# Four half units per expert job beside the first layer, and a larger TensorE share with more blocks for the experts beside the last attention

## The chip, the cores and the metric

The kernel runs on one core of a Trainium2 chip. The metric is the device time of one execution in microseconds. Before the change the median of three runs is 14575.84 us (14560.78 to 14577.56).

Each engine works through its own queue in the order in which the program was written: TensorE (PE; its weight loads are shown apart as PEld), VectorE (DVE), ScalarE (ACT), GpSimd (POOL), and SyncE (SP), which here issues nearly all the DMAs. An instruction that must wait holds up everything behind it on its engine.

## The reference

The input x has 4 entries of 32 x 96 tokens with 256 channels, all in float32. An entry therefore has 3072 tokens, and there are 12288 in all. What is computed:

```python
x = x + conv(group_norm(x))              # layer 0: two Mamba blocks, one along the 96, one along the 32
t = tokens(x)                            # (4, 3072, 256)
n = layer_norm(t)                        # additive attention within an entry:
h = tanh(n @ Wt [:, :, None] + n @ Wx [:, None] + bh)     # 3072 x 3072 x 32 of each entry
t = t + softmax(h @ Wa + ba) @ n
y = layer_norm(t)                        # expert layer:
gates = top2_softmax(graph_attention(y @ W_gat, edges))   # 1048576 edges over all 12288 tokens
for e in range(4):
    t = t + gates[..., e] * (gelu(y @ W1[e] + b1[e]) @ W2[e] + b2[e])   # 256 -> 512 -> 256
```

The product with the gates comes last. So an expert's output for a token (before its gate) can be computed as soon as that token's attention is done, kept in DRAM, and added when the gates are known.

## The kernel before

**Stages.** The order of the work on PE, ACT, DVE and POOL is written out by hand: Python generators are stepped in turn, and the order in which they emit instructions is the order in each engine's queue. First layer 0 of entry 0 runs alone. Then layer 0 of entries 1 to 3 runs beside the attention of entries 0 to 2. Then the attention of entry 3 runs beside the sorting and counting of the graph's edges (`Edges.sort`) and the first expert work (`Experts.early`). Last comes `tail`: the rest of the graph and of the experts.

**Columns, slots, blocks.** The attention (`Attention.units`) does one column at a time: ACT takes a tanh of 128 x 3072 (L1036), and PE multiplies it with Wa two columns later (L1009, the scores). There are three tanh buffers, so a tanh waits until the scores of the one three columns earlier are done. Eight columns make a unit of 32 queries; then an exponential, transposes and the product with the values follow. An entry has 768 columns. Layer 0 works in blocks of 384 tokens with 48 slots, one slot per column (`Layer0.run`). In each column the generators are stepped in two halves.

**A unit of expert work** is 512 tokens (a block, 24 in all, 6 per entry) by one expert; 96 in all. PE multiplies with W1 in four parts of 128 features, two matmuls each, then a GELU follows, and PE multiplies with W2. There are three places for it.

*`Beside`* works beside layer 0, on entries 0 and 1. A job is three half units (256 tokens each) of one expert and takes one block of layer 0; the table `PRODUCTS` says in which slot the two halves of a hidden product are issued, `GELU` in which slot the one GELU over all three (128 x 3072) is, `OUTPUTS` where the products with W2 are. Each product writes to the same single PSUM bank (`bank`, tile `ex`); DVE empties it in the next slot. The expert's weights and tokens lie in the key and query buffers (`krep`, `qsel`) that the attention will need for the next entry, so a job can start only while those are free. `choose` takes a job at the end of a block, if the entry's attention is past column 12, the keys of the next entry aren't asked for, and the tokens are of an entry that is normalized and older than the one whose attention runs. An entry has 12 half blocks and 4 experts: 16 jobs of three.

*`Experts.early`* works beside the last attention. It takes what `Beside` left of entries 0 to 2, two units of one expert at a time, with one GELU per unit (128 x 2048). It is a generator that yields after each small piece what that costs in the planner's microseconds (0.95 for a hidden matmul, 1.85 for a part of an output, 2.0 for the GELUs, 4.0 for a change of the expert). The loop in `whole` grants a credit in each column:

```python
us_t = min(us_t, SLOT_US) + SLOT_US - att.extra
```

where `att.extra` is what the attention's own tail steps cost in this column (0.7, 0.4 and 2.9 in three of eight). The credit first pays for one batch of the edge counting products (8 x 0.11), then for pieces of expert work as long as it is positive. `early` starts once entry 2 is wholly normalized, some 17 columns into the last attention. After the attention the pair that has begun is ended.

*`tail`* does the remaining units, and among them the graph: 384 row gathers by POOL, scores, scatter products (L1666) of 120 groups, and the gates of each quarter (entry) in the order 2, 0, 3, 1. Its planner lays everything out in half steps, six to a unit; it counts a half step with a unit as 2.7 us and one without as 0.5, a gather as 1.6 and a group as 2.0. For a block whose outputs were kept, the outputs of all four experts are read back (1 MB for half a block) and added with their gates (L1995), in blocks spaced by 2 or 3 times two half steps once its gates are ready.

The lines of the profile that matter: L1824 and L1835 (products of `Beside`), L1830 (its GELU), L1811 and L1816 (DVE emptying its bank), L1910 and L1918 (products of `early`, with `krep`, and of `tail`, with `w`), L1954 (GELU of `early`), L1992 (GELU of `tail`), L1265 (gathers) and L1601 (POOL's waits for DVE's marks that pace them).

Of the kernel before, what the change touches and what calls it, by code (L numbers as in the profile page):

```python
# [26 lines left out]
P = 128  # L27
# [4 lines left out]
KC = C // P  # L32
# [34 lines left out]
KO_BUFS = 2  # L67
SLOT_US, PRODUCT_US = 1.2, 0.11
EU, EG = 32, 2
# [771 lines left out]
class Attention:  # L841
# [4 lines left out]
    def __init__(self, ctx, tc, ident, a, x1, x2, xn2T, tab_s, tab_a, keys, l0):  # L846
# [30 lines left out]
        self.extra, self.entry, self.col, self.asked, self.normed = 0.0, 0, 0, 0, 0  # L877
        self.now, self.reduces, self.more, self.tc = None, False, [], tc
        self.mark = const.tile([P, 1], F32, tag="mark", name="mark")
# [320 lines left out]
    def after(self, b, t0=0, t1=NT):  # L1200
# [7 lines left out]
        for j in range(j0, N):  # L1208
# [27 lines left out]
            if b < B - 1:  # L1236
                nc.sync.dma_start(self.tab_e[:, n0:n0 + CT, :], hb)
            nc.sync.dma_start(self.tab_a[b][:, j * CT:(j + 1) * CT, :], db)
            if j == NT // CT - 1:
                self.normed = b + 1  # L1240
# [509 lines left out]
class Beside:  # L1750
# [4 lines left out]

    PRODUCTS = {0: (0, 0), 3: (0, 1), 5: (1, 0), 8: (1, 1), 10: (2, 0), 12: (2, 1)}
    GELU = 14
    OUTPUTS = {15: (0, 0), 17: (0, 1), 20: (1, 0), 23: (1, 1), 26: (2, 0), 29: (2, 1)}

    def __init__(self, ctx, tc, a, l0, att, xn2T, dram):  # L1760
# [6 lines left out]
        self.half = TB // 2  # L1767
        n = TOK // self.half // 3
        self.jobs = [(b, e, j) for b in range(B - 2) for e in range(NEXP) for j in range(n)]
        self.kept, self.done, self.job, self.there = {}, [], None, None  # L1770

    def units(self):

        halves = {(2 * (b * TOK // TB) + 3 * j + k, e) for b, e, j in self.done for k in range(3)}
        return [(i, e) for i in range(NBLK_X) for e in range(NEXP)
                if (2 * i, e) in halves and (2 * i + 1, e) in halves]

    def choose(self, last):
# [8 lines left out]
        place = att.krep[(att.entry + 1) % 2]  # L1787
        self.w1, self.w2 = expert_places(place)
        rest = att.qsel[(att.entry + 1) % 2]
        self.xt, self.b2 = rest[:, :KC * self.half].rearrange("p (k m) -> p k m", k=KC), rest[:, KC * self.half:]  # L1790
        if self.there != (att.entry, e):
            self.there = att.entry, e
            load_expert(self.nc, self.a, e, self.w1, self.w2)
            self.nc.sync.dma_start(self.b2, self.a["b2_rep"][:, e, :])
        self.first = 2 * (b * TOK // TB) + 3 * j
        self.fetch(0)

    def fetch(self, k):
        m = (self.first + k) * self.half
        self.nc.sync.dma_start(self.xt, self.xn2T[:, :, m:m + self.half].rearrange("k p m -> p k m"))  # L1800

    def __call__(self, slot, last):
        nc = self.nc
        if self.job:
# [3 lines left out]
            if slot - 1 in self.PRODUCTS:  # L1808
                k, f2 = self.PRODUCTS[slot - 1]
                for f in (2 * f2, 2 * f2 + 1):  # L1810
                    nc.vector.tensor_scalar(self.h[:, k, f, :], self.ps[:, f % 2, :],  # L1811
                                            self.b1[:, e, f:f + 1], None, ALU.add)
# [18 lines left out]
            if slot in self.OUTPUTS:  # L1831
                k, q = self.OUTPUTS[slot]
                self.ps = self.bank()
                for f in range(FC):
                    nc.tensor.matmul(self.ps[:, 0, :], self.h[:, k, f, q * P:(q + 1) * P],  # L1835
                                     self.w2[:, f, :], start=(f == 0), stop=(f == FC - 1))
# [14 lines left out]
class Experts:  # L1851
# [3 lines left out]
    def __init__(self, ctx, tc, x2, xn2T, gates, out, dram, beside=None):  # L1855
# [5 lines left out]
        self.kept, self.done = (beside.kept, beside.units()) if beside else ({}, [])  # L1861
        self.xts, self.turn = {}, {}

# [57 lines left out]

    def early(self, units, a, place):

# [6 lines left out]
        now = None  # L1930
        pairs = []
        for e in range(NEXP):
            mine = [u for u in units if u[1] == e]
            pairs += [mine[n:n + 2] for n in range(0, len(mine), 2)]
        for n, pair in enumerate(pairs):
            hs, e = [], pair[0][1]
            if e != now:
                now = e
                load_expert(nc, a, e, w1, w2)
                nc.sync.dma_start(b2, a["b2_rep"][:, e, :])  # L1940
                self.fetch(pair[0][0])
                yield 4.0
            for i, _ in pair:
# [280 lines left out]
def whole(tc, a, dram, out):  # L2224
# [12 lines left out]
    with ExitStack() as ctx:  # L2237
        actx, lctx, ectx = ExitStack(), ExitStack(), ExitStack()
        with tc.manual_schedule(engines={E.PE, E.Activation, E.DVE, E.Pool}):
# [8 lines left out]
            def steps():  # L2248
# [22 lines left out]
                while True:  # L2271
# [128 lines left out]
```

## Time and profile before

| | |
|---|---|
| median of three runs | 14575.84 us |
| profiled execution | 14585.4 us, span of its instructions 14583.6 us |
| busy in the span | PE 78%, DVE 72%, ACT 84%, POOL 62% |
| first tanh of the attention of entries 0, 1, 2, 3 | at 2154, 5155, 8284, 11296 us |
| end of the last tanh | 13647 us |
| first unit of the tail | 13733 us |
| the four quarters' sums in the tail | 13860, 13976, 14191, 14404 us |
| tanh (L1036) | 3072 of 2850 ns, 8658 us |
| scores (L1009) | 49152 matmuls, 4925 us |
| GELU of a job (L1830) | 25 of 2774 ns, 25 table loads of 1283 ns |
| GELU of `early` (L1954) | 22 of 1909 ns, 11 table loads |
| stores of a job's outputs | 150 of 128 KB |
| hidden products of `early` and of `tail` (L1910) | 352 and 592 |

A matmul in float32 stands in the trace as two. "Busy" is the time in which an engine executes; the idle time before an instruction is put down to the one that released it. In a window's row, the engines' busy times stand in the order PE, PEld, DVE, ACT, POOL, with the number of instructions in brackets, then the granted clock of TensorE, the share of DMA time and the rate.

### The profile page before, as it was taken

The numbers are of one execution on the slowest core, as the hardware profiler recorded it, in microseconds if no ns is written. First come the engines' busy times: TensorE is split into PE (matmuls) and PEld (weight loads), VectorE is DVE, ScalarE is ACT, GpSimd is POOL, SyncE is SP. The second block draws the span as 40 slices with busy tenths as digits, with TensorE's granted clock in tenths as the row PEclk, the third lists the DMA queues.
The fourth block names the chain that finished last, engine by engine and source line by source line (L and its number), as shares of the span: only waits on it lengthen the run. The fifth ranks groups of instructions, "written<-read, shape, count | busy, mean of one in ns | idle before, by whom it ended". The sixth has DMA issues, their size and how long they took to land.

```text
span 14583.6 us, 224819 instructions
## 1 busy us (share of the span) xinstructions
PE 11354.8 (78%) x86704; PEld 5155.9 (35%) x86704; DVE 10484.9 (72%) x15217; ACT 12282.5 (84%) x9676; POOL 9068.8 (62%) x7108
## 2 busy tenths in 40 slices
PE   5667766777777767888887687778877788888889
PEld 2333332222222333333333233333333333443466
DVE  7888887777777877777777777757776785333376
ACT  3445559999999889999998899999999999999522
POOL 5777767777777667767776677747774003653273
PEclk8898988888888889999998899999999999999999
DMA  6777764444444444445454444434543100000233
GB/s 207 225 229 231 231 207 145 148 147 152 151 152 155 145 147 151 153 150 158 153 155 147 145 152 153 154 107 152 158 153 116 41 22 19 12 16 16 58 105 124
DMA packets 1199840, 1984.20 MB, mean 136 GB/s; under 512 B 418596, under 2 KB 646436, under 8 KB 1193636
## 3 DMA queue, kind: packets, MB, share of 16 engines
q1 hardware_dynamic: 1168036, 1963.77, 42.6%
q0 software_dynamic: 30720, 5.96, 0.7%
q8 instruction: 682, 11.17, 0.3%
q14 instruction: 402, 3.29, 0.1%
HBM read 1859.14 MB, written 110.18 MB: 135 GB/s over the span
## 4 chain that ended last, share of the span: by engine, by line
ACT 39%; PE 25%; DVE 19%; issue 8%; POOL 7%; DMA 2%; SPq 1%; DVEq 0%; another core or an unknown queue 0%; POOLq 0%; ACTq 0%
ACT th L1036 28%; PE pe L1009 9%; ACT dA L470 6%; PE pv L1122 4%; DVE h L508 4%; DVE h L503 3%; DVE dB L483 3%; POOL h L515 3%; PE po L1918 2%; PE ph L1910 1%; ACT pr L1104 1%; PE py L534 1%; PE pz L577 1%; DVE acc L302 1%; PE ptw L1113 1%
## 5 line engine op out<-in xcount | busy, mean ns | idle before, releaser
L1036 ACT ACTIVATE th<-krep,qsel 128x3072 f32<-128x3072 f32 x3072 | 8657.8, 2850 | 280.8 <-PE pe L1009 266.3
L1009 PE MATMUL pe<-th,wa_blk 128*32 128x384 f32 x49152 | 4925.3, 529 | 940.0 <-ACT pr L1104 700.1
L515 POOL TENSOR_TENSOR h<-h,bC 128x768 f32<-128x768 f32 x2048 | 3763.0, 1838 | 2663.6 <-DVE h L508 2196.9
L508 DVE TENSOR_TENSOR_SCAN h<-dA,dB 128x384 f32<-128x384 f32 x3008 | 2706.6, 941 | 902.3 <-ACT dA L470 671.2
L1009 PEld LDWEIGHTS pe<-th,wa_blk 128*32 128x32 f32 x49152 | 1466.6, 115 | 3413.3 <-issue 1861.8
L483 DVE TENSOR_TENSOR dB<-bB,dtu 128x768 f32<-128x768 f32 x1912 | 1811.0, 947 | 206.9 <-ACT dtu L558 135.9
L522 POOL TENSOR_TENSOR h<-h 128x768 f32<-128x768 f32 x752 | 1412.9, 1879 | 53.6
L534 PE MATMUL py<-h,ident 128*128 128x384 f32 x2176 | 952.7, 570 | 485.1 <-POOL h L515 484.6
L470 ACT ACTIVATE dA<-dt,t_A 128x380 f32<-128x380 f32 x2048 | 1120.7, 570 | 240.6 <-DVE h L508 157.0
L1122 PE MATMUL pv<-xn,pT 128*32 128x257 f32 x18432 | 1156.8, 401 | 213.8 <-DVE pT L1115 213.0
L470 ACT ACTIVATE dA<-dt,d_A 128x372 f32<-128x372 f32 x2048 | 1106.8, 563 | 170.8 <-DVE h L508 90.5
L503 DVE TENSOR_TENSOR_SCAN h<-dA,dB 128x768 f32<-128x768 f32 x544 | 947.5, 1751 | 146.6 <-ACT dA L470 95.2
L1181 POOL TENSOR_SCALAR sf<-sel,f 128x32 f32<-128x32 f32 x384 | 137.0, 381 | 1241.8 <-ACT f L1177 1144.0
L1122 PEld LDWEIGHTS pv<-xn,pT 128*32 128x32 f32 x18432 | 598.9, 115 | 846.0 <-DVE pT L1115 369.6
L1097 DVE TENSOR_REDUCE nb<-pe 128x1 f32<-128x768 f32 x384 | 364.2, 948 | 719.0 <-PE pe L1009 707.4
L523 POOL TENSOR_TENSOR h<-h 128x384 f32<-128x384 f32 x752 | 790.0, 1051 | 59.0
L524 POOL TENSOR_TENSOR y<-y,h 128x384 f32<-128x384 f32 x752 | 777.0, 1033 | 59.0
L534 PEld LDWEIGHTS py<-h,ident 128*128 128x128 f32 x2176 | 427.6, 213 | 952.7 <-POOL h L515 723.8
L1113 PE MATMUL ptw<-ident,pr 128*128 128x128 f32 x2304 | 461.6, 316 | 306.5 <-DVE pT L1115 129.3
L1115 DVE COPY pT<-ptw 128x512 f32<-128x512 f32 (+1 forms) x768 | 417.9, 544 | 336.6 <-PE ptw L1113 315.6
L1265 POOL DMA_INDIRECT gd<-tab_a,di x480 | 492.0, 1025 | 160.7 <-issue 156.3
L1113 PEld LDWEIGHTS ptw<-ident,pr 128*128 128x128 f32 x2304 | 297.9, 160 | 773.8 <-issue 280.5
(329 smaller groups left out, 15094.8 us busy)
## 6 DMA issues: line engine op xcount, KB each, us to landing
bB<-bc SPq DMA_DIRECT2D x2048, 384.0 KB
bC<-bc SPq DMA_DIRECT2D x2048, 384.0 KB
x<-x SPq DMA_DIRECT2D x321, 128.0 KB
all<-kept SPq DMA_DIRECT2D x40, 1024.0 KB
kept<-ko SPq DMA_DIRECT2D x43, 512.0 KB
xt<-xn2T SPq DMA_DIRECT2D x41, 512.0 KB
qsel<-xn2T SPq DMA_DIRECT2D x75, 256.0 KB
kept<-eo SPq DMA_DIRECT2D x150, 128.0 KB
```

What stands on the lines that cost most here:

```text
L470: nc.scalar.activation(inner(dA[:, s * T:(s + 1) * T] if alone else self.dA[s][:, :T]), inner(blk["dt"][:, e, :]), AF.Exp, scale=blk["w"][ ...
L483: nc.vector.tensor_tensor(dB, blk["bB"].pop(j), z["dtu"].unsqueeze(1).to_broadcast([P, SB, T]), ALU.mult)
L503: nc.vector.tensor_tensor_scan(flat(h), dA[:, :SB * T], flat(dB), 0.0, ALU.mult, ALU.add)
L508: nc.vector.tensor_tensor_scan(h[:, s, :], self.dA[s][:, :T], dB[:, s, :], 0.0, ALU.mult, ALU.add)
L515: nc.gpsimd.tensor_tensor(h, h, blk["bC"].pop(j), ALU.mult)
L522: nc.gpsimd.tensor_tensor(h0, h0, h1, ALU.add)
L523: nc.gpsimd.tensor_tensor(h0[:, 0, :], h0[:, 0, :], h0[:, 1, :], ALU.add)
L534: nc.tensor.matmul(z["py"], self.ident, h[:, s, :], start=(i == 0), stop=(i == DS - 1))
L1009: nc.tensor.matmul(pe[q * QU:(q + 1) * QU, j, :KQ // 2], self.wa[:, k, :], th[:, c0:c0 + KQ // 2], start=(k == 0), stop=(k == NK - 1))
L1036: nc.scalar.activation(th, s["krep"], AF.Tanh, bias=s["qsel"][:, col:col + 1])
L1113: nc.tensor.transpose(pt[:, (i - i0) * P:(i - i0 + 1) * P], pr[:, i * P:(i + 1) * P], self.ident)
L1122: nc.tensor.matmul(pv[q * QU:(q + 1) * QU, :C + 1], pT[:, i, q * QU:(q + 1) * QU], s["xn"][:, q * NK + i, :], start=(i == 0), stop=(i == N ...
```

## The change

A job of `Beside` does four half units instead of three. The fourth's hidden values lie in the part of the key buffer behind the weights (`spare`, 1024 per partition), with a GELU of its own right behind the first. The tables of slots are new: 8 hidden products in slots 0 to 15, GELU in 17, 8 outputs in slots 18 to 27. An entry makes 12 jobs instead of 16.

`SLOT_US`, the credit of a column of the last attention, goes from 1.2 to 1.4. `early` starts with the last attention itself, and takes its units in three ranges: entries 0 to 2, then blocks 18 and 19, then 20 and 21 of the last entry. It takes a pair only when its tiles are normalized (`att.tiles`, new), and otherwise gives up its turn for some columns (9.0). The order of the experts is turned around from one range to the next. At the end it ends the pair at hand, or nothing if it was waiting.

```diff
-SLOT_US, PRODUCT_US = 1.2, 0.11
+SLOT_US, PRODUCT_US = 1.4, 0.11
...
 # Attention.after
             nc.sync.dma_start(self.tab_a[b][:, j * CT:(j + 1) * CT, :], db)
+            self.tiles = b * NT + (j + 1) * CT
...
 # Beside
-    PRODUCTS = {0: (0, 0), 3: (0, 1), 5: (1, 0), 8: (1, 1), 10: (2, 0), 12: (2, 1)}
-    GELU = 14
-    OUTPUTS = {15: (0, 0), 17: (0, 1), 20: (1, 0), 23: (1, 1), 26: (2, 0), 29: (2, 1)}
+    HALVES = 4
+    PRODUCTS = dict(zip((0, 1, 3, 5, 8, 10, 12, 15), ((k, f) for k in range(4) for f in range(2))))
+    GELU = 17
+    OUTPUTS = dict(zip((18, 19, 20, 23, 24, 25, 26, 27), ((k, q) for k in range(4) for q in range(2))))
...
-        n = TOK // self.half // 3
+        n = TOK // self.half // self.HALVES
...
+        self.spare = place[:, KC * FF + FC * C:].rearrange("p (f m) -> p f m", f=FC)
...
-        self.first = 2 * (b * TOK // TB) + 3 * j
+        self.first = 2 * (b * TOK // TB) + self.HALVES * j
...
+    def hidden(self, k, f):
+        return self.h[:, k, f, :] if k < 3 else self.spare[:, f, :]
...
-                if f2 and k < 2:
+                if f2 and k + 1 < self.HALVES:
                     self.fetch(k + 1)
             if slot == self.GELU:
-                h = self.h.rearrange("p k f m -> p (k f m)")
-                nc.scalar.activation(h, h, AF.Gelu)
+                for h in (self.h.rearrange("p k f m -> p (k f m)"),
+                          self.spare.rearrange("p f m -> p (f m)")):
+                    nc.scalar.activation(h, h, AF.Gelu)
...
 # Experts.early
-        pairs = []
-        for e in range(NEXP):
-            mine = [u for u in units if u[1] == e]
-            pairs += [mine[n:n + 2] for n in range(0, len(mine), 2)]
+        pairs, PER = [], NBLK_X // B
+        n, own = PER * (B - 2), PER * (B - 1)
+        order = sorted(range(NEXP), key=lambda e: -sum(i < n and k == e for i, k in units))
+        for i0, i1 in (0, own), (own, own + 2), (own + 2, own + 4):
+            for e in order:
+                mine = [u for u in units if u[1] == e and i0 <= u[0] < i1]
+                pairs += [mine[n:n + 2] for n in range(0, len(mine), 2)]
+            order = order[::-1]
+        there = lambda pair: att.tiles >= (pair[-1][0] + 1) * TB // P
         for n, pair in enumerate(pairs):
             hs, e = [], pair[0][1]
+            while not there(pair):
+                if self.closing:
+                    return
+                yield 9.0
...
-            if n + 1 < len(pairs):
+            if n + 1 < len(pairs) and there(pairs[n + 1]):
                 self.fetch(pairs[n + 1][0][0])
...
 # whole
-                    if units is None and att.entry == B - 1 == att.normed:
+                    if units is None and att.entry == B - 1:
                         units = late["units"] = ex.early(
-                            [(i, e) for i in range(NBLK_X - NBLK_X // B) for e in range(NEXP)
-                             if (i, e) not in ex.done], a, att.krep[B % 2])
+                            [(i, e) for i in range(NBLK_X) for e in range(NEXP)
+                             if (i, e) not in ex.done], a, att.krep[B % 2], att)
...
+            late["ex"].closing = True
             while begun:
                 begun = next(late["units"], None)
```

More of the change, by code (lines that the diff above doesn't have):

```diff
@@ L877, in __init__ @@
         self.extra, self.entry, self.col, self.asked, self.normed = 0.0, 0, 0, 0, 0
-        self.now, self.reduces, self.more, self.tc = None, False, [], tc
+        self.now, self.reduces, self.more, self.tc, self.tiles = None, False, [], tc, 0
         self.mark = const.tile([P, 1], F32, tag="mark", name="mark")
@@ L1772, in units @@
     def units(self):
-        halves = {(2 * (b * TOK // TB) + 3 * j + k, e) for b, e, j in self.done for k in range(3)}
+        halves = {(2 * (b * TOK // TB) + self.HALVES * j + k, e)
+                  for b, e, j in self.done for k in range(self.HALVES)}
         return [(i, e) for i in range(NBLK_X) for e in range(NEXP)
@@ L1810, in __call__ @@
                 for f in (2 * f2, 2 * f2 + 1):
-                    nc.vector.tensor_scalar(self.h[:, k, f, :], self.ps[:, f % 2, :],
+                    nc.vector.tensor_scalar(self.hidden(k, f), self.ps[:, f % 2, :],
                                             self.b1[:, e, f:f + 1], None, ALU.add)
@@ L1834, in __call__ @@
                 for f in range(FC):
-                    nc.tensor.matmul(self.ps[:, 0, :], self.h[:, k, f, q * P:(q + 1) * P],
+                    nc.tensor.matmul(self.ps[:, 0, :], self.hidden(k, f)[:, q * P:(q + 1) * P],
                                      self.w2[:, f, :], start=(f == 0), stop=(f == FC - 1))
@@ L1861, in __init__ @@
         self.kept, self.done = (beside.kept, beside.units()) if beside else ({}, [])
-        self.xts, self.turn = {}, {}
+        self.xts, self.turn, self.closing = {}, {}, False
     def open(self, ctx, w):
@@ L1920, in output, with early @@
             yield po
-    def early(self, units, a, place):
+    def early(self, units, a, place, att):
         nc = self.nc
```

## The prediction

> **What bounds the kernel now.** I read the slices first (the span in 40 parts of 365 us), then the busy time of each engine inside single blocks and columns, then the waits.
>
> ```profile
> PE   5667766777777767888887687778877788888889
> DVE  7888887777777877777777777757776785333376
> ACT  3445559999999889999998899999999999999522
> POOL 5777767777777667767776677747774003653273
> ```
>
> Digits are tenths of a slice. Three stages follow the lead: slices 7 to 31, layer 0 beside attention, with ACT at 9; slices 32 to 37, the last entry's attention, ACT 9, PE 8; and the last three, where ACT falls to 2 and PE is at 8 to 9. The change moves expert work from the third stage into the first two. So the question is what a unit (512 tokens by one expert) frees in the tail, and what it costs where ACT already sets the pace.
>
> Whole blocks of 48 columns, two without an expert job and two with one (columns: stretch, its length, then busy time and count of PE, PEld, DVE, ACT, POOL; granted clock, DMA share, GB/s):
>
> ```profile
> 2426.53:2607.05 180.52, 130.49 (x1180) 49.51 (x1184) 141.82 (x188) 178.55 (x136) 137.18 (x101) 0.88 0.50 149
> 2607.05:2787.45 180.40, 128.41 (x1166) 50.01 (x1158) 138.69 (x180) 178.42 (x136) 136.34 (x97) 0.89 0.45 148
> 5271.50:5459.15 187.65, 148.26 (x1262) 66.54 (x1254) 144.41 (x198) 184.21 (x138) 135.72 (x97) 0.92 0.46 149
> 5650.55:5838.06 187.51, 149.59 (x1262) 66.64 (x1254) 144.68 (x198) 184.19 (x138) 135.87 (x97) 0.91 0.46 151
> ```
>
> A job of three half units adds 18 to 21 us to PE but only 7.1 to 7.5 us to the block; ACT is 98 to 99% busy either way. Slots 18 to 28 of the third of these blocks:
>
> ```profile
> 5341.50:5380.00 38.50, 31.64 (x271) 14.84 (x274) 33.68 (x50) 37.14 (x29) 31.10 (x25) 0.93 0.51 167
> ```
>
> Four stretches of 8 columns of the last attention, the third with a pair of GELUs; the whole of it; and two of its waits (total, times, longest):
>
> ```profile
> 12586.68:12609.46 22.78, 20.93 (x226) 9.37 (x226) 8.16 (x15) 22.78 (x10) 13.84 (x21) 1.00 0.04 3
> 13060.84:13083.61 22.77, 20.01 (x222) 9.62 (x222) 7.72 (x14) 22.77 (x10) 13.66 (x21) 1.00 0.06 7
> 13362.46:13391.79 29.33, 21.94 (x206) 9.42 (x210) 3.95 (x9) 29.27 (x16) 1.37 (x4) 0.94 0.06 19
> 13391.79:13414.54 22.75, 20.84 (x208) 9.29 (x201) 5.05 (x10) 22.75 (x10) 0.00 (x0) 0.92 0.04 13
> 11296.00:13647.00 2351.00, 2030.88 (x20608) 909.75 (x20608) 1179.51 (x2193) 2266.40 (x938) 701.10 (x1057) 0.97 0.09 22
> ```
> ```profile
> ACT th L1036 <- PE pe L1009: 70.7, 56, 7.1
> PE ph L1910 <- DVE h L1949: 64.5, 45, 4.2
> ```
>
> The floor of 8 columns is 22.76 us, ACT without a gap, and PE is then busy for 20.0 to 20.9 us: some 2 us free. A GELU pair makes it 29.3. The whole takes 2351 us.
>
> The tail: until the third quarter's gates, until the last scatter product, and after it:
>
> ```profile
> 13733.00:14190.00 457.00, 396.63 (x1482) 293.77 (x1483) 320.96 (x798) 136.24 (x167) 343.26 (x373) 0.94 0.34 90
> 14190.00:14398.00 208.00, 177.13 (x630) 128.03 (x629) 150.75 (x377) 56.05 (x69) 127.82 (x150) 0.92 0.44 140
> 14398.00:14583.60 185.60, 177.12 (x626) 119.07 (x624) 100.82 (x225) 38.49 (x54) 0.37 (x1) 0.99 0.32 111
> ```
>
> In the first two, PE, DVE and POOL all work at 60 to 87%: the units share time with the graph. Only in the last 186 us is there nothing but units, 12 at 13.8 us each (starts of the hidden products: 14402.5, 14416.3, ... 14554.8).
>
> **Counts.** The groups of lines give them: 150 kept stores of jobs, two a half unit, make 75 half units in 25 jobs, so 37 whole units; 44 x 8 hidden products (each shown twice) make 22 early units; 148 tail GELUs make 37. Sum 96 = 24 x 4. Of the 25 jobs, 13 have their GELU in the second entry's attention (5326 to 7622) and 12 in the third's (8456 to 10664). After the change 12 jobs cover an entry: the second's attention does 12 and must pass its thirteenth, since the next entry isn't normalized; the third's does 12. All 24 run: 48 units. That needs the second entry normalized by column 19 of the third attention; its last gate product starts in column 16 (8376.8).
>
> Early units follow from the credit. Per 8 columns it is 8 x SLOT_US minus 0.7 + 0.4 + 2.9 for the attention's own steps and 0.075 for the tile's: 5.5 now, 7.1 after. The 232 count products take 0.88 each, 204 in all. A pair costs 2 x 7.6 + 2 + 2 x 7.4 = 32, a change of expert 4. Now: 94 x 5.5 - 204 - 14 = 299, nine pairs, the rest of 22 after the attention. After: 96 x 7.1 - 204 - 32 = 446, fourteen pairs, and one more ended behind: 30 units, six of them in blocks 18 and 19, whose tiles are there from column 282. The tail keeps 96 - 48 - 30 = 18 instead of 37.
>
> **Jobs beside layer 0.** One job less gives back 7.5 us. Each of the 24 gets a second GELU of 1024 wide: 2774 ns for 3072 makes some 1.0 us, with the table already loaded. PE gets 4 bursts of 8 matmuls at 2.0 us, 4 x 0.476 + 2 x 0.414 = 2.7 us go to DVE, one fetch of 256 KB and two stores of 128 KB to SP's queue, all under ACT by the block rows (PE has 38 us a block free, DVE 43). SP's fetch waits for the matmuls that still read its tile, with layer 0's broadcasts queued behind it, three times a job for two; DVE waits for broadcasts 45.7 us in the whole run now, so this stays small. What isn't covered is order: products at slots 0, 1 and outputs at 18 to 20 and 23 to 27 are now in neighbouring slots, and the bank they share is one buffer, so PE waits at each for DVE to empty it, with scores and transposes queued behind. Four bursts more (8 us) fall between slots 18 and 27, where the row above leaves PE 6.9 us free and scores start up to 7 us after their tanh; the third tanh buffer allows two columns of 3.75 less 1.5 of scores, 6. Bounds: 0.3 us of stall (nothing but the fetch) and 5.5 (most of the 8 us). Now a job block has 3.2 us of ACT idle before its tanhs against 1.5 without. I take 2.2, nearer to that row: 24 x 3.2 - 7.5 = +69 us; bounds 24 x 1.3 - 7.5 = +24 and 24 x 6.5 - 7.5 = +149.
>
> **The larger share.** Ten more units (28 for 18) inside the attention. On ACT that is five pairs: 2 x 1.9 + 2 x 1.28 = 6.4 us by the rows; by the stretches 29.3 - 22.8 = 6.5. So 5 x 6.6 = +33 us that nothing covers. The Trainium skill (ScalarE: Activation LUTs, What ACT_TABLE_LOAD costs) speaks more strongly against it: a switch costs its 1283 ns load and a drain of about 1380 ns, which would make 5 x 9.1 = 46. The stretch shows no room for the drains.
>
> On PE, 1.6 of credit per 8 columns is 1.6 x 13.8/15 = 1.5 us against the 2 us free. Cover is nearly used up, so the 70.7 us that tanh now waits for scores must grow. Low bound: nothing. High bound: PE, freed of ACT, needs 2031 busy, 193 of waits that are not for tanh or exp (DVE's evacuation of h, 64.5, is the largest), 145 for ten units at the tail's 14.5 and 90 more such waits: 2459, +108, and with the GELUs +141. I take 45: three of these four stretches are at the floor, with PE waiting for tanh and not the other way, which is nearer to the low end. The earlier start (column 0 for 17) sets a 1 MB expert load and its wait into columns where tanh already waits: 5 us. Ten units bring DVE 10 x (4 x 0.744 + 2 x 0.69) = 44 us, under ACT. Sum +83, bounds +38 and +146. A second page (Perfetto Trace Analysis, Identifying the Most-Contended Engine) says that LDWEIGHTS busy, not matmul busy, tells PE's headroom. That is 9.4 of 22.8 us here; by it the 45 would be 0. I stay with the idle time, since the bursts wait in order.
>
> **The tail.** The plan is in half steps, six per unit, and costs units at 2.7 us and gathers at 1.6. With 18 units, it is the same as now up to half step 108: 16.5 units lie before the third quarter's gates anyway (14190), and at 4.4 us a half step from there, half step 108 falls near 14220. So 457 us of the tail don't shrink. Behind lie 85 of 384 gathers and 27 of 120 groups. POOL's rows there:
>
> ```profile
> L1265 POOL DMA_INDIRECT gs<-tab_e,si x58 | 62.2, 1073 | 14.7 <-issue 14.7
> L1265 POOL DMA_INDIRECT gs<-tab_s,si x48 | 53.2, 1108 | 11.8 <-issue 11.8
> L1601 POOL COPY seen<-mark 1x1 f32<-1x1 f32 x44 | 13.3, 302 | 28.4 <-DVE mark L1600 26.9 <-DVE ko L1982 0.9 <-issue 0.3
> ```
>
> With the issue gaps a gather takes (62.2 + 53.2 + 26.5)/106 = 1.34 us; 85 of them and 66 paces of 0.30 are 134 us: 14364 with the last group's 10. If the third quarter's six blocks (16 adds of 0.484 each and 3 MB of DMA, some 75 us with their groups) hold the paces back, 64 gathers follow them and the end is 14406. Before: 14398. Then come the last gates (27), six blocks at 9 us and the store (6): 14451 to 14493, against 14583.6. I take -108, and -10 for 2 units less of work between attention and tail. Sum -118, bounds -100 and -143. Of 19 units (262 us of PE) less than half comes back.
>
> **Sum.** +69 + 83 - 118 = +34 us against the profiled execution's 14585.4 (span 14583.6), which is 9.6 above the median of the runs, 14575.84. Against the median: 14610.
>
> **Rivals.**
> Attention becomes PE-bound. PE's order leaves ACT waiting in both early stages: +149 + 146 - 118 = +177, 14753; from the forecast halfway there, 14680. For: 2 us free of 22.8, 1.5 taken. Against: half of the stretches show no lag at all. Chance 0.22.
> Faster, by the tail: it gives back all PE time, 19 x 13.8 = 262 + 10. Then 69 + 83 - 272 = -120: 14456. For: PE is at 86% in all three windows. Against: the gathers' plan above. It decides from 181 us on (69 + 83 + 29). Chance 0.13.
> The cover holds in both early stages: 24 + 38 - 118 = -56: 14520. For: 18 us of PE per job cost 2 us beyond ACT's own so far. Chance 0.20.
> That fewer units move than said (one job lost costs 2 units, some 27 us of tail) I give no share of its own: the counts have one answer.
>
> **How the numbers follow.** My forecast has 0.45; its own range is 14560 to 14670. About 0.2% (29 us) is what a measurement of this kernel tells from no change. Of the forecast 0.13 is within it, 0.32 above; of the covered case 0.17 is below and 0.03 within; the tail's case is below, the PE-bound case above. Faster 0.30, same 0.16, slower 0.54. For 8 in 10 I leave out the tail's end and the worst stalls: 14480 to 14740.
>
> **What would show it.** 96 half units and 48 units of jobs, 30 early GELUs, 18 x 4 tail GELUs; job blocks of about 191 us and a second GELU without a load; an attention of 2434 us with tanh's wait for scores at 115 or more; third gates still 457 us after the tail's first unit, the last scatter product some 195 us behind them, and then only six blocks. The prediction is wrong if job blocks stay at 188.5, if the attention's wait stays at 70, or if the gap between third and last gates falls below 140 us.

## The result: 2.4% slower, and the profile after

The changed kernel takes 14916.83 us (median of four runs, 14912.76 to 14919.73), the kernel before in the same comparison 14570.85 us. The ratio is 1.0237, with a 95% interval of 1.0224 to 1.0249. The forecast was 14610 with a range up to 14740. So the sign was right, and the size was wrong by some 300 us.

The slices of the changed kernel, as shown for the kernel before:

```profile
PE   5766767777777677778877678778877888999882
DVE  7888887787777777777777777756777676343276
ACT  3445559999999899989898899999999899999620
POOL 5777767777776666666666666646665002664174
```

ACT now has 8 in between its 9s, and PE did not rise to 9 for that: whoever ACT waits for is not full. Cut at the first tanh of the second attention, the first and the last tanh of the last attention and the end of the span, the two profiled executions differ so:

| stage | before | after | difference | forecast |
|---|---|---|---|---|
| jobs beside layer 0 (two attentions) | 6141.5 | 6465.0 | +323.5 | +69 |
| last attention | 2350.8 | 2402.9 | +52.1 | +83 |
| tail | 936.7 | 895.3 | -41.4 | -118 |
| whole span | 14583.6 | 14917.6 | +334.0 | +34 |

(The small rest lies before the second attention.) Two terms failed, and both in the same direction: the jobs by 254 us and the tail by 77.

**Blocks with a job.** The first two job blocks of the changed kernel, 48 columns each, each from one column later than the windows shown before, then ten columns of the first, slots 19 to 28:

```profile
5277.55:5475.11 197.56, 155.22 (x1296) 72.88 (x1292) 145.81 (x207) 185.89 (x139) 136.75 (x98) 0.91 0.45 143
5475.11:5677.53 202.42, 162.21 (x1313) 76.24 (x1309) 149.07 (x209) 186.69 (x140) 136.38 (x100) 0.90 0.47 145
...
5351.12:5395.91 44.79, 34.95 (x271) 19.09 (x272) 34.19 (x53) 37.75 (x29) 26.84 (x18) 0.93 0.43 133
```

The same two blocks took 187.7 and 191.4 us before; the forecast was about 191 on the mean. PE has 7 to 11 us more work in them and is still idle for 40. The same ten columns took 38.6 us before (5345.1 to 5383.7) and now take 44.8, with ACT busy for 37.2 and 37.8: nearly all of the difference is ACT standing still.

**Whom they wait for.** Waits between the two entries' first tanhs, 5154 to 11290 us (total, times, longest). Of the kernel before:

```profile
ACT th L1036 <- PE pe L1009: 143.6, 129, 5.0
PE ex L1835 <- DVE eo L1816: 7.0, 9, 1.5
PE ex L1824 <- DVE eh L1811: 1.8, 8, 0.6
```

and of the changed kernel, where L1831 are the hidden products, L1843 the outputs, L1818 and L1823 the DVE operations that empty their bank, and L1838 the GELUs:

```profile
ACT th L1036 <- PE pe L1009: 377.5, 297, 5.0
PE ex L1843 <- DVE eo L1823: 257.7, 119, 6.8
PE ex L1831 <- DVE eh L1818: 59.4, 31, 3.1
PE ex L1843 <- ACT eh L1838: 47.4, 24, 3.0
DVE eo L1823 <- DMA kept<-eo: 30.4, 19, 3.1
```

PE waits 258 us for DVE to empty the bank of an output, where it had waited 7: 119 waits, five a job. Six of its outputs have one in the slot before (those of slots 19, 20 and 24 to 27), and in the trace all of these wait but the one of slot 25 (and once that of slot 20). The matmuls behind it in PE's queue are the scores, and the tanhs wait 234 us longer (252 up to the end of the stage at 11619). PE also waits 47 us for the GELU ahead of the output of slot 18, where it had waited 11. The last line is a wait that the prediction did not name at all: the staging tile of the outputs is one SBUF buffer too, and DVE must wait until its store has left.

One wait at slot 19, in the first job block (start, length, engine, line and operation; in brackets the idle time before it and its releaser):

```profile
5344.91 1.04 ACT L1838 ACTIVATE krep<-krep 128x1024 f32<-128x1024 f32 x1
5345.06 1.99 PE L1843 MATMUL ex<-krep,eh 128*128 128x256 f32 x8 [2.14 <-ACT eh L1838]
5350.12 1.06 ACT L470 ACTIVATE dA<-dt,t_A 128x380 f32<-128x380 f32 x2
5350.77 1.80 DVE L508 TENSOR_TENSOR_SCAN h<-dA,dB 128x384 f32<-128x384 f32 x2 [4.63 <-issue]
5352.61 0.95 DVE L483 TENSOR_TENSOR dB<-bB,dtu 128x768 f32<-128x768 f32 x1
5353.48 0.42 DVE L1823 TENSOR_TENSOR eo<-ex,qsel 128x256 f32<-128x256 f32 x1
5353.95 3.65 PE L1843 MATMUL ex<-krep,eh 128*128 128x256 f32 x8 [5.61 <-DVE eo L1823]
```

The output of slot 18 is done at some 5347, but DVE empties its bank only at 5353.5: two scans and a product of layer 0 (L508, L483) stand ahead in DVE's order. The scans read dA, which ACT makes from 5350.1 on, behind the two GELUs of slot 17, a table load and a tanh. (The profile names no releaser for them; that they waited for dA is read from the times.) The trace has this order ahead of slot 19's wait in all 24 jobs; these waits add up to 106 of the 258 us. So the wait is made of the orders of three engines, and the GELU has a part in it. The burst behind it is slower too, 3.65 us for eight matmuls where that of slot 18 took 1.99.

**The tail**, cut like before: until the third quarter's sum, until the last one's, and after it:

```profile
14104.90:14576.60 471.70, 391.24 (x1474) 291.90 (x1473) 344.63 (x850) 134.55 (x164) 350.57 (x376) 0.92 0.35 93
14576.60:14831.20 254.60, 76.85 (x256) 62.58 (x255) 147.18 (x412) 5.59 (x14) 143.37 (x196) 0.64 0.36 114
14831.20:14917.60 86.40, 0.33 (x2) 0.00 (x0) 59.70 (x143) 1.88 (x3) 0.00 (x0) 0.53 0.52 183
```

The first stretch is 472 us (457 before) and the last 86 (179 before), nearly as forecast. But the middle one, 214 us before, takes 255 and not 195, although PE, DVE and POOL are each busy for less than 60% of it.

### The profile page after: what moved, and what is told of

It is laid out like the page before. It is cut to its first block, busy times and chain, and to the rows that moved or that the text cites. A ratio compares the mean times of both kernels' runs of the same rounds, so it can differ in the third digit from the quotient of the medians.

```text
span 14917.6 us, 225482 instructions
## 1 busy us (share of the span) xinstructions
PE 11388.4 (76%) x86848; PEld 5203.3 (35%) x86848; DVE 10517.0 (71%) x15403; ACT 12274.5 (82%) x9608; POOL 9095.4 (61%) x7150
## 4 chain that ended last, share of the span: by engine, by line
PE 32%; ACT 29%; DVE 21%; issue 8%; POOL 7%; DMA 3%; SPq 1%; DVEq 0%; POOLq 0%; ACTq 0%
ACT th L1036 20%; PE pe L1009 11%; PE pv L1122 5%; ACT dA L470 5%; DVE h L508 4%; DVE dB L483 3%; POOL h L515 3%; DVE h L503 3%; PE ex L1843 2%; PE po L1926 2%; PE pz L577 1%; PE ph L1918 1%; PE py L534 1%; PE ex L1831 1%; PE px L296 1%
## 5 line engine op out<-in xcount | busy, mean ns | idle before, releaser
L508 DVE TENSOR_TENSOR_SCAN h<-dA,dB 128x384 f32<-128x384 f32 x3008 | 2705.0, 940 | 854.1 <-ACT dA L470 557.8
L483 DVE TENSOR_TENSOR dB<-bB,dtu 128x768 f32<-128x768 f32 x1912 | 1810.0, 947 | 207.7 <-ACT dtu L558 134.2
L1266 POOL DMA_INDIRECT gd<-tab_a,di x480 | 499.2, 1040 | 158.0 <-issue 153.0
```

The source lines that it names most:

```text
L483: nc.vector.tensor_tensor(dB, blk["bB"].pop(j), z["dtu"].unsqueeze(1).to_broadcast([P, SB, T]), ALU.mult)
L508: nc.vector.tensor_tensor_scan(h[:, s, :], self.dA[s][:, :T], dB[:, s, :], 0.0, ALU.mult, ALU.add)
```

## Experiments

Ratios are to the kernel before on the same chip. Stages are meant as in the table above.

### One part at a time

The kernel before with the new `Beside` alone:

```diff
 # before, and
+    HALVES = 4, its slots, spare, hidden, second GELU
     SLOT_US = 1.2, Experts.early and whole as before
```

> The kernel before with the jobs of four half units alone (the share 1.2, the old early units). Theory A (the neighbouring slots of the jobs cost the time): layer 0 beside the attention of entries 1 and 2 keeps its whole loss, 5154 to about 11619, +323 us; the last attention goes back to 2351; the tail has 26 units, its graph ends as before (671 us after the first unit) and only the six last blocks follow, so it gives back some 85 us: in all about +240, 14810. Theory B (jobs and early units hurt each other, or the share is what costs): under +100, below 14670.

Measured 14816.08 us, ratio 1.0164 (1.0144 to 1.0185). The stage of the jobs took 6478.5 us (+337), with the same waits as in the changed kernel (256.7 us for the outputs' bank); the last attention took 2338.7, and the tail 849.5, 87 less, with 26 units in it.

The changed kernel with the old `Beside`:

```diff
 # after, and
-    HALVES = 4, its slots, spare, hidden, second GELU
+    Beside as before
```

> The changed kernel with the jobs of before (three half units, 25 jobs). Theory A: layer 0 back at 6142 us for entries 1 and 2; the last attention +52 as in the changed kernel; about 27 to 28 units in the tail, whose graph ends as before, so some 80 us come back: 14540 to 14570, by 0 to 30 us faster than before. Theory B (the share costs): over 14620.

Measured 14581.9 us, ratio 1.0006 (0.9996 to 1.0015): no change. The last attention costs 62 us more (2413.3), the tail gives 69 back (867.4), also with 26 units. So the larger share alone is near balance, and the jobs alone lose 1.6%. The rest of the 2.4% comes only where both are together, and it lies in the tail: it gives back 87 us with the one and 69 with the other, but 41 with both, where the sum would be 156. The section on the tail below shows what is in the way.

### The slots

The products of the changed kernel with a free slot behind each but one, and the same amount of work:

```diff
-    PRODUCTS = dict(zip((0, 1, 3, 5, 8, 10, 12, 15), ...
-    GELU = 17
-    OUTPUTS = dict(zip((18, 19, 20, 23, 24, 25, 26, 27), ...
+    PRODUCTS = dict(zip((0, 2, 4, 6, 8, 10, 12, 13), ...
+    GELU = 15
+    OUTPUTS = dict(zip((16, 18, 20, 22, 24, 26, 28, 30), ...
```

> The changed kernel, its hidden products in slots 0, 2, 4, 6, 8, 10, 12 and 13, the GELU in 15, the outputs in every second slot from 16 to 30. All the work is the same. Theory A: a job's block goes from 203 to some 192 us, PE's wait for the emptied bank (258 us now) to under 60, and the time to about 14670. Theory C (the volume of the fourth half unit costs, wherever it lies): blocks stay at 200 to 203, the time within 40 us of 14917.

Measured 14708.53 us, ratio 1.0090 (1.0070 to 1.0111). The stage takes 6257.2 us, 208 less than in the changed kernel. Its waits:

```profile
ACT th L1036 <- PE pe L1009: 256.8, 216, 8.0
PE ex L1843 <- DVE eo L1823: 0.4, 1, 0.4
PE ex L1831 <- DVE eh L1818: 1.7, 7, 0.3
```

The wait for the bank is gone, 0.4 us for 257.7, with every matmul of the fourth half unit still there. But the GELU moves too, from slot 17 to 15, and PE's wait for it falls from 47.4 us to 9.4. What is left over the kernel before is 116 us.

The opposite, the kernel before with three half units and neighbouring slots:

```diff
-    PRODUCTS = {0: (0, 0), 3: (0, 1), 5: (1, 0), 8: (1, 1), 10: (2, 0), 12: (2, 1)}
-    GELU = 14
-    OUTPUTS = {15: (0, 0), 17: (0, 1), 20: (1, 0), 23: (1, 1), 26: (2, 0), 29: (2, 1)}
+    PRODUCTS = {0: (0, 0), 1: (0, 1), 3: (1, 0), 5: (1, 1), 8: (2, 0), 10: (2, 1)}
+    GELU = 17
+    OUTPUTS = {18: (0, 0), 19: (0, 1), 20: (1, 0), 23: (1, 1), 24: (2, 0), 25: (2, 1)}
```

> The kernel before, its jobs of three half units moved into neighbouring slots: products in 0, 1, 3, 5, 8, 10, GELU in 17, outputs in 18, 19, 20, 23, 24, 25. No work is added. Theory A: a job's block goes from 190 to 196 or more, +150 us or more in all. Theory C: it stays at 190, the time within 40 us of 14571.

Measured 14790.0 us, ratio 1.0146 (1.0126 to 1.0167): no work added, and yet 228 us more in the stage (6370.0).

```profile
ACT th L1036 <- PE pe L1009: 334.8, 274, 5.8
PE ex L1835 <- DVE eo L1816: 174.3, 75, 5.9
PE ex L1824 <- DVE eh L1811: 61.4, 26, 3.7
```

75 waits are three for each of the 25 jobs: of the four outputs with one in the slot before, again all but that of slot 25. The GELU moves here as well, from slot 14 to 17, and PE's wait for it goes from 11.4 us to 59.0. This and the run before show the same from both sides: the placing of a job's products and its GELU is worth 208 to 228 us, whatever the number of half units. What the bank alone is worth they do not show.

### Is it the wait for the bank, or too many matmuls at once?

Neighbouring slots do two things: PE must wait for DVE, and bursts follow each other closely. Three runs were made to part these two. Two outputs into the two halves of one bank, to spare one wait in two:

```diff
-                self.ps = self.bank()
+                if q == 0:
+                    self.ps = self.bank()
...
-                    nc.tensor.matmul(self.ps[:, 0, :], ...
+                    nc.tensor.matmul(self.ps[:, q, :], ...
```

> The changed kernel in its own slots; the two outputs of a half unit go to the two halves of the bank, so that the second needn't wait for DVE to empty the first. The density of work is the same, 4 of the 8 waits are gone. Theory A1 (PE standing before the full bank costs): PE's wait for eo falls from 258 to under 140, tanh's wait for scores from 378 to under 290 (same stretch), the time to 14800 or less. Theory A2 (the density of bursts behind slot 17 costs, with or without the wait): the wait moves, tanh's stays above 340, the time above 14870.

Measured 14934.79 us, ratio 1.0231 (1.0210 to 1.0251). PE waited for DVE 120 times and 261.5 us, as without the edit (119 times and 257.7). So it did not take the wait away, and tells nothing on the question.

Bursts of half the length in the same slots; two of the four parts of each output's sum are left out:

```diff
-                for f in range(FC):
+                for f in range(2):
```

> The changed kernel in its own slots, but an output product of a job sums only two of the four parts of the hidden values (the other half of that product is left out): each of the 8 bursts falls from 2.0 to 1.0 us, the waits for DVE to empty the bank stay. Theory A1 (PE standing before the full bank until DVE's place in the order comes): tanh's wait for scores in 5154 to 11290 stays above 320 us (378 now), the time above 14840. Theory A2 (too many bursts behind slot 17): it falls under 250, the time under 14790.

Measured 14896.77 us, ratio 1.0207 (1.0187 to 1.0228). The stage falls by 30 us only, to 6435.0.

```profile
ACT th L1036 <- PE pe L1009: 350.7, 304, 5.5
PE ex L1843 <- DVE eo L1823: 329.9, 121, 7.7
```

With half the matmuls PE waits longer for DVE (329.9 us), not less: what PE saves in a burst it spends in front of the next. Shorter bursts give 30 us back, free slots 208. That speaks against the density of the bursts and for the waits. A run with neighbouring slots and without the wait for the bank, which would show it outright, was not made, since the edit above did not remove it; nor was one that moves the GELU alone.

Bursts of double length in the spaced slots; each part of the sums is added twice:

```diff
 # spaced_slots, and
-                for f in range(FC):
+                for f in range(2 * FC):
```

> The spaced slots, with every output product of a job done over its four parts twice (the output counts the sum double): 8 bursts of 4.0 us for 2.0, 16 us more on PE per job, and no neighbouring slots. Theory A1: PE's free time takes most of it, a block goes from 194 to at most 200, the time at most 14830. Theory A2 (PE's work between the scores is what costs): it passes the tanh buffers' room, blocks at 203 or more, the time above 14900.

Measured 14886.16 us, ratio 1.0200 (1.0179 to 1.0220). The stage takes 6421.2 us, 164 more than with spaced slots, or 6.8 us a job for some 16 us more of PE work. No bank is waited for here. So the volume has a price as well, between the two expectations: 6.8/16, some 0.43 us for 1 us of PE. That fits what spaced slots leave, 116 us and the 7.5 of the job that is gone: 24 second GELUs are 25 us, and 24 x 8 us of additional bursts at 0.43 are 82, together 107 of 123.

### The tail

The tail's gathers without paces once the units are over:

```diff
             if half in calls:
-                gr.pace()
+                if half < 6 * len(units):
+                    gr.pace()
```

> The changed kernel; POOL's gathers of the tail are no longer paced by DVE's marks in the half steps without a unit. Theory T (the marks tie the last 109 gathers to DVE's place among the adds, where POOL stood still for up to 88 us): from the third to the last quarter's sum 255 us becomes 190 or less, and the time 14850 or less. Theory U (POOL's own time for the gathers, 1.34 us each, sets it): it stays above 235, the time within 25 us of 14917.

Measured 14907.98 us, ratio 1.0212 (1.0192 to 1.0233). Third to last sum took 233.3 us instead of 255.0. So the paces alone were not the cause. The gathers now came first and the adds behind them. POOL waited for DVE's `v` (L1638) instead, 78.5 us in two waits, and DVE stood still for 49 us in front of `n` (L2344), the flag for edges that were left over, which needs a reduction by POOL. I took the flag for the cause and moved it ahead of the tail:

```diff
 # free_gathers, and in whole, before tail(...)
+            nc.gpsimd.partition_all_reduce(top, late["ed"].lost, P, bass_isa.ReduceOp.max)
+            nc.vector.tensor_scalar(n, top, 0.0, None, ALU.max)
```

> As the changed kernel with unpaced gathers, and the small reduction of the lost edges' flag (POOL, then DVE), which stood 49 us in DVE's way behind the unpaced gathers, is done ahead of the tail. Theory T (POOL stands still while DVE adds kept blocks, and then has 80 gathers left): from the third to the last quarter's sum 255 us becomes 185 or less, the time 14860 or less. Theory U (order on DVE itself: adds and groups one behind the other): it stays above 215.

Measured 14902.17 us, ratio 1.0211 (1.0190 to 1.0231); third to last sum 225.3 us. The standstill moved to another operation, so the flag was not its cause:

```profile
DVE ko L1999 <- issue: 31.7, 1, 31.7
```

Two more runs: the spaced slots and the unpaced gathers together, and the two outputs in one bank on top of that:

```diff
 # spaced_slots with the edit of free_gathers; then also with that of shared_bank
```

> Spaced slots and unpaced gathers together. By theories A and T the two gains add: 14708 - 65 = 14640. If they overlap, 14700.

> Spaced slots, unpaced gathers and the halves of the bank shared by the two outputs. In the spaced slots PE's wait for the bank was 0.4 us, so by theory A1 the third part adds nothing: as spaced_free, about 14640, which isn't better than before.

Measured 14699.49 us, ratio 1.0069 (1.0049 to 1.0090), and 14709.6 us, ratio 1.0074 (1.0057 to 1.0091): neither beats the kernel before. Third to last sum took 237.4 and 217.9 us.

What sets it was to be seen by counting the gathers (L1266) in the first 100 us behind the third sum and in the rest. The changed kernel, POOL's busy time and count for this line alone:

```profile
14576.60:14676.60 100.00, 20.98 (x20) 0.59 0.73 256
14676.60:14831.20 154.60, 98.34 (x89) 0.68 0.12 22
```

and the kernel before:

```profile
14190.60:14290.60 100.00, 63.66 (x59) 0.95 0.50 159
14290.60:14404.20 113.60, 50.84 (x47) 0.89 0.38 122
```

In the changed kernel DVE does 125 adds (L2012) in the first 100 us, 16 to a block, and POOL gets only 20 gathers in. The planner has placed some two beside each block: it spaces blocks by six half steps there, and six half steps without a unit count 3 us for it. One number changed in it:

```diff
-            us += HALF_US if half < 6 * len(units) else 0.5
+            us += HALF_US if half < 6 * len(units) else 1.7
```

> The changed kernel with one number of the tail's planner changed: a half step without a unit counts as 1.7 us, not 0.5. Between the sums of the third and the last quarter the changed kernel takes 255.0 us; in the first 100 of them VectorE does the third quarter's six blocks of adds, and GpSimd issues only 20 of the 108 gathers that are left. Theory P, the plan's price: a block of adds has six half steps, which the plan counts as 3 us without units, so it lays two gathers of 1.6 us beside adds that take 16 us on the chip. At 1.7 a block has 10 us and six gathers. Some 45 to 60 gathers then come in the first 100 us, and the last sum stands 185 to 215 us behind the third: 40 to 70 us less, a time of 14850 to 14880. Theory Q, the gathers or VectorE beside them are slow by themselves: moving gathers beside the adds slows the adds by as much, the 255 us stay within 10, and the time stays at 14917 within 20.

Measured 14870.77 us, ratio 1.0193 (1.0176 to 1.0210). Third to last sum takes 202.3 us, and the gathers and the whole stretch are

```profile
14581.50:14681.50 100.00, 58.13 (x52) 0.69 0.60 198
14681.50:14783.80 102.30, 61.38 (x56) 0.68 0.29 88
```
```profile
14581.50:14783.80 202.30, 78.28 (x256) 63.05 (x255) 144.87 (x396) 5.60 (x14) 144.53 (x177) 0.69 0.44 143
```

52 gathers come in the first 100 us, not 20, and the stretch is 52 us shorter with the same 108 gathers: those 52 us were the plan's doing, as theory P had it.

The standstills of DVE were measured by themselves, in a stretch of small operations added behind the last unit, first alone, then beside 36 gathers:

```diff
+        two_inputs(20)
+        one_input(20)
+        gr.pace()
+        for g in (2, 3, 4):
+            for c in range(g * GP, (g + 1) * GP):
+                gr.gather(7, g, c, "s")
+        for _ in range(3):
+            two_inputs(20)
+            one_input(20)
```

> The changed kernel with a stretch added behind the last unit, which measures and computes nothing that is used: 20 small VectorE operations with two inputs in SBUF (128 x 24) and 20 with one, alone; then 36 gathers by GpSimd without paces, and beside them three times 20 and 20 of the same operations. If the gathers themselves slow VectorE, as the standstills of 32 and 49 us in the two runs without paces suggested, the operations come some 0.24 us apart alone and 1.2 us or more apart beside the gathers (both kinds, or only those with two inputs), and the added stretch is 36 x 1.3 = 47 us or longer. If something else held VectorE there, they come 0.24 us apart in both stretches, and the 120 operations are over after 30 us.

Measured 15001.92 us, in one run. DVE's timeline (start, length, operation, how many in a row, idle time before and its releaser); gathers are issued from 14947.0 to 14991.9:

```profile
14942.36 4.21 DVE L2149 TENSOR_SCALAR small<-small 128x24 f32<-128x24 f32 x20
...
14956.04 4.35 DVE L2153 TENSOR_TENSOR small<-small 128x24 f32<-128x24 f32 x20
...
14978.68 0.18 DVE L2153 TENSOR_TENSOR small<-small 128x24 f32<-128x24 f32 x1 [1.22 <-DVE small L2153]
...
14980.78 0.18 DVE L2149 TENSOR_SCALAR small<-small 128x24 f32<-128x24 f32 x1 [1.21 <-DVE small L2153]
...
14995.49 0.18 DVE L2149 TENSOR_SCALAR small<-small 128x24 f32<-128x24 f32 x1 [1.21 <-DVE small L2149]
```

Both expectations were half right. Alone (but for one stop of 3.9 us at a branch of the program, L2367) and beside the first 15 gathers the operations come some 0.22 us apart. From 14966 on they mostly come 0.7 or 1.4 us apart, those with one input as well as those with two, and each is still 0.18 us long.

### A smaller share

The old `Beside`, and a credit between the two:

```diff
 # share_alone, and
-SLOT_US, PRODUCT_US = 1.4, 0.11
+SLOT_US, PRODUCT_US = 1.3, 0.11
```

> The changed kernel with the jobs of before and a share of 1.3 in place of 1.4. Theory F (only units behind the last scatter product, some seven beyond the 87 us that the last gates and blocks take, are time in the tail; one unit costs the last attention 5.6 us): about 28 early units and 31 in the tail, attention +30, tail -75 to -85: 14520 to 14540, 0.2 to 0.4% faster than before. If each early unit costs the attention as much as it frees, 14570 to 14590.

Measured 14543.98 us against 14594.06 for the kernel before in the same comparison, ratio 0.9963 (0.9948 to 0.9977): 0.4% faster than the kernel before, as theory F expected. The last attention takes 2392.2 us (+41, for the +30 expected), the tail 851.5 (-85), with 27 early units and 32 in the tail:

```profile
14238.50:14442.50 204.00, 181.86 (x649) 132.00 (x648) 139.49 (x352) 56.17 (x69) 124.60 (x148) 0.92 0.37 111
14442.50:14552.80 110.30, 101.94 (x365) 68.89 (x363) 83.52 (x193) 24.75 (x34) 0.49 (x1) 0.99 0.49 163
```

Third to last sum is 204 us with units in it, and the units behind it fill PE for 102 of 110 us. In the changed kernel, with no unit left there, the adds of the last blocks alone take 86, and with 26 units in the tail (jobs alone) it was 92. So ten units fewer took only 6 us from the end of the tail, while the stretch before it grew from 204 us to 255: that is why the gains of the two parts do not add.

## Why the prediction was wrong

**Jobs beside layer 0: +69 forecast, +323.5 measured. The failed term is the stall of 2.2 us a job, bounded at 5.5.** The other two terms held: the second GELU took 1041 ns and loaded no table ("some 1.0"), and there were 24 jobs. By the forecast's own formula a job cost (323.5 + 7.5)/24 = 13.8 us instead of 3.2, so the stall was 12.8. The mechanism was named ("PE waits at each for DVE to empty it, with scores and transposes queued behind") but priced as another one. I took the four additional bursts, 8 us, against 6.9 us of free PE time as the upper bound, which is a price for volume. It was misread as well: by the tables, slots 18 to 27 get eight outputs for three, so five bursts more, and only two of these are of the fourth half unit. The wait for a bank depends on where DVE's emptying stands in DVE's own order, as at slot 19 above, and it strikes every neighbouring pair but one, those of the old half units included: three_neighbours pays it with no burst added. The spaced slots part the two. They leave (116 + 7.5)/24 = 5.1 us a job, which less the GELU is 4.1 of stall, inside the bounds. The other 8.7 us, 208 us in all, went with the placing: PE's waits for the bank (257.7 + 59.4 us became 0.4 + 1.7) are the largest part of what went, its wait for the GELU (47.4 became 9.4) a smaller one; how many of the 208 us belong to each stays open.

No row of the kernel before priced it. Its outputs were two or three slots apart and waited 7.0 us in 9 cases, 1.5 at most; between neighbours the mean is 257.7/119 = 2.2 us, five times a job, or 10.7 us. With nothing near in the trace, the bound had to be worked out from the distance between the orders of the engines.

**The larger share: +83 forecast, +52 measured.** The five pairs of GELUs were right: 28 units had theirs inside the attention, 18 before. The stall was not 45. Waits in the last attention, 11619 to 14022:

```profile
ACT th L1036 <- PE pe L1009: 92.2, 77, 9.8
PE ph L1918 <- DVE h L1966: 88.1, 61, 8.8
```

Tanh waits 92.2 us for scores against 70.7: +21.5, where 115 or more was what would have shown the forecast. 33 + 21.5 is 54.5, close to the 52. The Trainium skill's rule on headroom (Perfetto Trace Analysis, Identifying the Most-Contended Engine; it names MFU, the share of the peak rate, beside the busy time of weight loads) made the 45 a 0 by the weight loads; the measured 21 lies in the middle. The skill's drain of some 1380 ns at a change of table (ScalarE: Activation LUTs, What ACT_TABLE_LOAD costs) would have made the pairs an estimated 46 and, with this wait, 67; the row's 33 agrees with the chip.

**The tail: -118 forecast, -41 measured. The failed step is "If the third quarter's six blocks ... hold the paces back, 64 gathers follow them and the end is 14406".** That was the upper bound, 216 us behind the third gates, of which I took 195. The chip took 255: the adds stood in front from the third sum on and for 100 us (125 adds are nearly eight blocks), not for 75 from half step 108 on, and 89 gathers followed, not 64. The tail had two units fewer than forecast, the last one's hidden products at 14554 us, so the plan was already at its cheap half steps when the third sum came at 14577. 25 gathers more at the 1.55 us at which they then came (13 in 20 us) are 39 us, just what is missing. The rest was nearly as worked out: 472 us until the third sum for 457, and 86 behind the last for 87 (the 27 of the gates, six blocks at 9 and the store, 6). Only the work between attention and tail stayed, at 83 us for 86, where -10 was forecast for two units less.

**Counts.** 96 half units and 48 units of jobs, as said. Early units were 32, not 30: two pairs are ended behind the attention, not one, as in the kernel before (18 inside, 22 in all). The tail had 16 units for 18.

**Rivals.** The PE-bound one had the right direction, and its "PE's order leaves ACT waiting" is what happened beside layer 0, at more than twice its +149; in the last attention hardly (+21.5). But PE is not bound: it is 79% busy in the stage of the jobs before (4864.65 of 6141.5 us) and after (5075.38 of 6465.0). It is not full, it waits in order. The one that decided for faster, by the tail, is refuted by the 41 us; the cover held in neither stage.

## What to carry to other kernels

In an order written by hand, the distance between a product and the operation that empties its only bank is a resource of its own: here two products into one bank wanted at least one slot of other work between them, and 40 us of idle PE time in a block did not pay for a missing one. To bound such a wait, follow both engines' orders from the emptying back to what stands ahead of it, and count all pairs, not only the added ones. Where a planner lays out the work, look up what it charges for an empty step before moving work out of it: the step may have been spaced by the work that is taken away.

## What the hardware showed beside that

VectorE fell behind beside gathers that GpSimd issued without pause. In vector_beside_gathers that began 18 us after the first gather and ended at 14997.6, 5.7 us after the last was issued; 34 operations took 32 us, where 34 x 0.22 = 7.5 were needed. In the kernels without paces it had stood still for 32 and 49 us; whether for the same cause, no run shows. A page of the Trainium skill (SBUF — State Buffer, SBUF: two separate sides) has VectorE and GpSimd share one pair of ports, which an instruction holds until its end: on VectorE's side one in a two-port mode, or one with two inputs in SBUF beside a GpSimd operation that reads SBUF. The runs do not look like that alone: the same operations beside the first 15 gathers lose nothing, and beside the later ones their own length does not change. That one input is hit as much as two decides nothing, since no run shows the mode. The cause stays open.
